# A new order for the start of a two-layer graph transformer: input loads on another queue, step 0 normalised row tile by row tile, neighbour flags by TensorE

## The chip, the cores and the metric

The kernel runs on one core of one Trainium2 chip. The metric is the device time of one execution in microseconds. TensorE is called PE in the profile, VectorE DVE, ScalarE ACT, GpSimd POOL and SyncE SP; SPq and ACTq are the parts of SyncE and ScalarE that issue transfers.

## The reference, cut to what matters

There are 64 graphs of 256 nodes with 512 features, and a 256x256 adjacency mask for each graph. Two layers follow each other, and each adds an attention over the neighbours to its input:

```
h = relu(layernorm(x));  x = x + L0(h, adj)     # 4 heads of 64; a node without a neighbour weighs all nodes alike
h = relu(layernorm(x));  x = x + L1(h, adj)     # a second layernorm inside (gamma, beta), 8 heads of 64, mask = adj or the diagonal
L0: softmax(where(adj, q k^T / 8, -max)) v @ Wo + bo         with q, k, v = h Wq, h Wk, h Wv
L1: softmax(where(adj | eye, q k^T / 8, -1e9)) v @ w_out^T + b_out   with q, k, v = h @ w_qkv^T
```

All values are float32; the mask comes as one byte per element.

## The kernel before

**Steps.** Two graphs are worked on at a time, so there are 32 steps of four row tiles of 128 nodes (`t`), and the 512 features are four chunks of 128 (`c`). All tiles of a step are 128 partitions by 512 elements for one row tile or one chunk.

**One step.** `load_h` brings x into the tile `h` (L476 for step 0, one load for each row tile; L478 for the others, one load of 1 MB) and the mask into `ad` (L480). `norm0` takes mean and variance of a row tile on DVE (`moments`, L547 and L548); with the last row tile, POOL works out one scale `r` and one offset `mr` for each row (`row_scales`, L555 to L559, a power of -0.5), and `scale_row` applies them. `transpose_h` turns the rows on PE, chunk by chunk, and the copy out of PSUM on ACT applies the relu (L619). `act_sums0` and `act_sums1` form four sums of blocks of the result on POOL. `project_qk` makes q and k with seven products of eight matmuls (called `n` = 1, 6, 5, 2, 7, 3, 4 in their order; a scheme with seven products in place of eight), which need sums of the weights too (`weight_sum`, L403). Each product is added up by DVE or ACT (`evacuate`, L630 to L642). The products 2 and 1, 4 and 7, 3 and 5 share a PSUM bank: product 4 is added into the bank of product 7, and only after that bank has been read. `project_v0` makes v for each row tile. `scores`, `mask_scores` (DVE, L807), `exponentials` (ACT, L812), `key_halves` (POOL, L820), `weigh` (PE, L829 and L849), `invert` (DVE, L859) and `normalise` (POOL, L876) are the attention of a pair of heads; the inverted sums go through eight small transfers (L871). `combine0` applies `Wo` to a row tile and adds x (tile `xt`, loaded by `load_x`, L485, with the bias added by `first_bias` on POOL). Layer 1 follows in the same way: `norm1`, `norm1_rest`, `scale_row`, `transpose_h` with gamma and beta, `project_qk`, `project_v1`, four pairs of heads, `combine1` and `store`.

**The neighbour flags.** `neighbours` reduces the mask to one flag for each node (L504). `spread_neighbours` spreads the flags over all partitions: one transfer writes them to DRAM, four bytes at a time (L511), and a second reads them back with a step of zero over the partitions (L513, tile `ne`). `masks` (POOL, L533 to L542) and the copies of products 3 and 4 (L706) use `ne`.

**The order.** Each piece of work is put on a list by `at(period, place, function)`; `at_dense` and `at_set` add a product at one place and its copy out of PSUM at the end of its slot. The list is sorted by `period * 6.13 + place`, and PE, DVE, ACT and POOL execute their instructions in just that order. SP is not among these four: its transfers are put in an order by the framework. Transfers issued by ACT (`nc.scalar.dma_start`) stand in ACT's list at their place. In what follows a place is counted from the start of the list of step 0: `load_h(0)` is at -0.43, `project_qk` of step 0 at 3.57 to 4.57, `load_h(1)` at 3.2, `load_x(0)` at 3.9, `norm0(1, t)` at 4.0, 4.2, 4.4 and 4.6, `project_qk` of step 1 at 5.5, and the first product of layer 1 of step 0 at 12.26. From there on each period has the same pieces of work.

**Loads of the weights.** `first_weights` loads Wq and Wk on SP (tile `wqk0`, four loads L428), and Wv, Wo, the two biases, gamma and beta on ACT. `weight_loads` loads 4 MB of layer-1 weights on ACT, at place 3.5 (four loads L455 into tiles called `wr`, which lie in the space of tiles that come later; one of them lies in the space of an `xt`). `weight_block` turns a quarter of such a load on PE, and DVE and ACT copy it (sixteen blocks, L461 and L466).

**Tiles.** A tile waits for its space until the tile that had it before is no longer read. There is one `h`, one `ad` and one `ne`, and there are two `xt`.

Of the kernel before, what the change touches and what calls it, by code (L numbers as in the profile page):

```python
# [8 lines left out]
FP = mybir.dt.float32  # L9
BF = mybir.dt.bfloat16  # L10
U8 = mybir.dt.uint8
I32 = mybir.dt.int32
AF = mybir.ActivationFunctionType
ALU = mybir.AluOpType

EPS = 1e-5
# [299 lines left out]
def fast_path(  # L316
# [19 lines left out]
    nc = tc.nc  # L336
# [38 lines left out]
    offdiag = const.tile([P, G, P], BF, name="offdiag")  # L375
    for g in range(G):
        nc.vector.tensor_scalar(offdiag[:, g, :], ident, -1.0, 1.0, op0=ALU.mult, op1=ALU.add)
    ones = const.tile([P, 32], FP, name="ones")
    nc.vector.memset(ones, 1.0)
    mhalf = const.tile([P, NT], FP, name="mhalf")  # L380
# [27 lines left out]
    def act_sums1(b, eng=nc.gpsimd):  # L408
        eng.tensor_tensor(b[:, 4], b[:, 2], b[:, 3], ALU.subtract)
        eng.tensor_tensor(b[:, 5], b[:, 2], b[:, 7], ALU.subtract)  # L410
        eng.tensor_tensor(b[:, 6], b[:, 1], b[:, 4], ALU.subtract)
# [13 lines left out]
    def first_weights():  # L425
        for i in range(2):
            for k, w in enumerate((wq, wk)):
                nc.sync.dma_start(  # L428
                    wqk0[:, 2 * i:2 * i + 2, :, k, :].rearrange("p j c o -> p (j c) o"),
                    w[:, i * H0:(i + 1) * H0].rearrange("(c p) o -> p c o", p=P),  # L430
                )
        nc.scalar.dma_start(wv0, wv.rearrange("(c p) o -> p c o", p=P))
        nc.scalar.dma_start(wo0, wo.rearrange("(c p) o -> p c o", p=P))
        for v, t in ((bo, bo_b), (b_out, bout_b)):
            nc.scalar.dma_start(t, bass.AP(tensor=v.tensor, offset=v.offset, ap=[[0, P], [1, D]]))
        gbr = sm.tile([2 * NC, P], FP, name="gbr", tag="inv", bufs=1)
        nc.scalar.dma_start(gbr[:NC], gamma.rearrange("(c p) -> c p", p=P))
        nc.scalar.dma_start(gbr[NC:], beta.rearrange("(c p) -> c p", p=P))
        return gbr
# [6 lines left out]
    def weight_loads():  # L446

        pair = act.tile([P, 2, 4, D], FP, name="wr", tag="oT1")
        blocks = [
            pair[:, 0], pair[:, 1],  # L450
            act.tile([P, 4, D], FP, name="wr", tag="v1"), io.tile([P, 4, D], FP, name="wr", tag="xt"),
        ]
        for n, wr in enumerate(blocks):
            src, r0 = (w_qkv, 4 * n) if n < 3 else (w_out, 0)
            nc.scalar.dma_start(wr, src[r0 * P:(r0 + 4) * P].rearrange("(r p) i -> p r i", p=P))  # L455
        return blocks

    def weight_block(wr, n, c):
# [46 lines left out]
            st["any"][:, rows], st["ad"][:, rows], axis=mybir.AxisListType.X, op=ALU.max  # L505
        )

    def spread_neighbours(s):

        row = dram.tile([NT, P], FP, name="row")  # L510
        nc.sync.dma_start(row.rearrange("t p -> p t"), S[s]["any"])  # L511
        ne = S[s]["ne"] = act.tile([P, T], FP, name="ne")
        nc.sync.dma_start(ne, bass.AP(tensor=row.tensor, offset=row.offset, ap=[[0, P], [1, T]]))  # L513

    def adjacency_turn(s):
        adb = S[s]["adb"]
# [43 lines left out]

    def scale_row(s, t):
        h, r, mr = S[s]["h"], S[s]["r"][:, t:t + 1], S[s]["mr"][:, t:t + 1]
        if s == 0 and t % 2:
            nc.vector.tensor_scalar(h[:, t, :], h[:, t, :], r, mr, op0=ALU.mult, op1=ALU.add)
        else:
            nc.scalar.activation(h[:, t, :], h[:, t, :], AF.Identity, bias=mr, scale=r)  # L566

    def norm0(s, t):
        st = S[s]
        if t == 0:  # L570
            st["mean"] = stat.tile([P, NT, 2], FP, name="mv0", bufs=2)
        moments(st["mean"], st["h"], t)
        if t == NT - 1:
            ve = stat.tile([P, NT], FP, name="ve0", bufs=2)
            nc.gpsimd.tensor_scalar(
                ve, st["mean"][:, :, 1], EPS, 1.0, op0=ALU.add, op1=ALU.mult
            )
            row_scales(s, ve)
# [29 lines left out]
    def transpose_h(s, lyr, c):  # L608
        st = S[s]
        if c == 0:  # L610
            st["hT"] = act.tile([P, NB + 1, HC, N], FP, name="hT")
        ph = mm_tile([P, G, N])
        pv = ph.rearrange("p g n -> p (g n)")
        for t in range(NT):
            nc.tensor.transpose(pv[:, t * P:(t + 1) * P], st["h"][:, t, c * P:(c + 1) * P], ident)  # L615
        b0, b1, step = B_OF[c // HC]
        dst = st["hT"][:, b0:b1:step, c % HC, :]
        if lyr == 0:
            nc.scalar.activation(dst, ph, AF.Relu)  # L619
        else:  # L620
            nc.scalar.activation(
                dst, ph, AF.Identity, bias=gb[:, 1, c:c + 1], scale=gb[:, 0, c:c + 1]
            )

    def evacuate(n, bank, region):

# [259 lines left out]
    def at(period, place, fn, *args):  # L886
        events.append((period * PERIOD + place, len(events), fn, args))
# [48 lines left out]
    for s in range(NSTEP):  # L936

        p = s - 2
        if s == 1:
            p -= 3.93 / PERIOD  # L940
        at(p - 1 if s != 1 else -2, 5.7 if s != 1 else 3.2, load_h, s)
        at(p, (2.9, 2.4)[s] if s < 2 else 0.2, adjacency_cast, s)
        for t in range(NT):
            at(p, 0.5 + 0.4 * t if s != 1 else 1.8 + 0.2 * t, norm0, s, t)
            at(p, 2.3 + 0.1 * t if s != 1 else 2.6 + 0.1 * t, scale_row, s, t)
        for g in range(G):
            at(p, (1.8, 2.7)[s] if s < 2 else 0.58 + 0.14 * g, neighbours, s, g)
        at(p, (1.81, 2.71)[s] if s < 2 else 0.75, spread_neighbours, s)
        at(p, (3.146, 3.584)[s] if s < 2 else 2.2, adjacency_turn, s)
        at(p, (3.3, 3.727)[s] if s < 2 else 2.75, masks, s)  # L950
        for c in range(NC):
            at(p, AT_C0 + 0.14 * (c // 2) + 0.001 * c, transpose_h, s, 0, c)
        at(p, AT_C0 + 0.1, lambda s=s: act_sums0(S[s]["hT"]))
        at(p, AT_C0 + 0.2, lambda s=s: act_sums1(S[s]["hT"]))
        at_set(p, AT_Q0 if s != 1 else 3.3, SET, project_qk, s, 0, 0)
        for t in range(NT):
            at_dense(p, AT_V0 + 0.14 * t, 0.14, project_v0, s, t)
        p = s - 1
        if s == 0:
            p -= 2.23 / PERIOD  # L960
        at(p, 1.0 if s else 0.0, load_x, s)
        at(p, 1.8 if s else 0.8, first_bias, s)
        for t in range(NT):
            at_dense(p, AT_C0 + 0.01 + 0.14 * t, 0.14, combine0, s, t)
            at(p, AT_C0 + 0.3 + 0.14 * t, norm1, s, t)
            at(p, (3.55, 3.7, 4.05, 4.2)[t], norm1_rest, s, t)
            at(p, 3.62 + 0.08 * t, second_bias, s, t)
            at(p, 4.5 + 0.1 * t, scale_row, s, t)

        for c in range(NC):  # L970
            at(p, AT_H1 + 0.0001 * c, transpose_h, s, 1, c)
        at(p, AT_C1 + 0.15, lambda s=s: act_sums0(S[s]["hT"]))
        at(p, AT_C1 + 0.5, lambda s=s: act_sums1(S[s]["hT"]))
        p = s
        at_set(p, 0.0, SET, project_qk, s, 1, 0)
        at_set(p, 1.0, SET, project_v1, s)
        at_set(p, 2.0, SET, project_qk, s, 1, 1)
        at(p, 4.55, lambda s=s: act_sums0(S[s]["oT1"], engine_of(s, 1, 1)))
        if s < NSTEP - 1:
            at(p, AT_C1 + 0.1, lambda s=s: act_sums1(S[s]["oT1"]))  # L980
            at_set(p, AT_C1, SETC, combine1, s)
            at(p, 6.3, store, s)
        else:
            at(p, AT_C1 + 0.4, lambda s=s: act_sums1(S[s]["oT1"], nc.vector))
            at_set(p, AT_C1, (1, 5, 2, 3, 6, 7, 4), combine1, s)
            for n, (i, j) in enumerate(((0, 0), (0, 1), (1, 1), (1, 0))):
                at(p, AT_C1 + (3, 6, 6, 7)[n] / 7, store_block, s, i, j)
# [1 line left out]
    gbr, blocks = [], []  # L989
    at(-3, 5.71, lambda: gbr.append(first_weights()))  # L990
    for i in range(4):
        at(-2, 2.75, weight_sum, nc.vector, wqk0, i)
    at(-2, 3.5, lambda: blocks.extend(weight_loads()))
    at(-2, AT_V0 + 0.2, lambda: gamma_beta(gbr[0]))
    for i in range(16):
        place = 3.3 - 3.93 + 1 / 7 - 0.0005 if i < 4 else 0.2 + 0.07 * i if i < 8 else 1.34 + 0.1 * (i - 8)
        at(-1, place, lambda i=i: weight_block(blocks[i // 4], i // 4, i % 4))
    for i in range(4):
        at(-1, 0.1 + 0.01 * i, weight_sum, nc.vector, wqkv1[:, :, :, 0, :], i)
        at(-1, 1.0 + 0.01 * i, weight_sum, nc.vector, wqkv1[:, :, :, 1, :], i)  # L1000
        at(0, 0.2 + i / 7, weight_sum, nc.vector, wqkv1[:, :, :, 2, :], i)
        at(0, 1.3 + 0.5 * i, weight_sum, nc.gpsimd, wo1, i)
    for _, _, fn, args in sorted(events, key=lambda e: e[:2]):
# [53 lines left out]
```

## Time and profile before

| | |
|---|---|
| median of 9 runs | 3429.93 us (3428.49 to 3436.54) |
| the profiled execution | 3429.1 us |
| its span (first to last instruction) | 3427.3 us |
| mean granted TensorE clock | 0.996 |
| PE busy | 3379.1 us, 99% of the span |
| DVE, ACT, POOL busy | 55%, 36%, 58% |

PE is busy almost everywhere. The execution's own time is 1.8 us more than its span. The windows show the granted clock in each stretch of time; 1.00 is full speed.

### The profile page before, as it was taken

The page shows a single profiled execution, that of the slowest core. Times are in us where ns is not written, and L with a number is a line of the kernel's source. Part 1 is how long each engine was busy: PE and PEld are TensorE (multiplying, and loading weights), DVE is VectorE, ACT ScalarE, POOL GpSimd, SP SyncE. Part 2 cuts the span into 40 slices and gives each one's busy share as a digit, 9 for nine tenths or more (in the row PEclk, how much of TensorE's full clock was granted, in tenths as well). Part 3 has the DMA queues.
Part 4 walks back from the last instruction along what each step waited for, and adds up shares of the span by engine and source line. Part 5 has one row for each costly group of instructions (what it writes and reads, how often), then busy time and mean ns, then how long its engine had stood idle before and what let it go on. Part 6 is the DMA issues. An engine that isn't in the chain of part 4 may idle for free.

```text
span 3427.3 us, 59200 instructions
## 1 busy us (share of the span) xinstructions
PE 3379.1 (99%) x22594; PEld 2625.1 (77%) x22594; DVE 1898.3 (55%) x3377; ACT 1245.0 (36%) x2197; POOL 1991.1 (58%) x1854
## 2 busy tenths in 40 slices
PE   7999999999999999999999999999999999999998
PEld 5787777877777877777777778777777777787766
DVE  4655555555565555555555655555555556555554
ACT  3433443333433334433334333344333443333421
POOL 4556665556655556655566555566555665555641
PEclk9999999999999999999999999999999999999999
DMA  4121111111112111111211112111111111111011
GB/s 134 42 58 51 34 47 56 56 57 52 35 45 58 58 52 34 47 56 56 57 52 34 46 57 58 53 33 47 56 56 57 54 33 46 57 58 51 21 42 38
DMA packets 169041, 174.42 MB, mean 51 GB/s; under 512 B 60712, under 2 KB 113456, under 8 KB 168752
## 3 DMA queue, kind: packets, MB, share of 16 engines
q1 hardware_dynamic: 165344, 164.67, 16.5%
q10 hardware_dynamic: 3408, 5.90, 0.5%
q8 instruction: 180, 2.95, 0.4%
q14 instruction: 109, 0.89, 0.1%
HBM read 86.51 MB, written 33.62 MB: 35 GB/s over the span
## 4 chain that ended last, share of the span: by engine, by line
PE 96%; DMA 1%; DVE 1%; POOL 1%; SPq 0%; issue 0%; ACT 0%; ACTq 0%; DVEq 0%; POOLq 0%
PE mm L696 34%; PE mm L737 11%; PE mm L762 11%; PE sc L794 10%; PE sc L829 10%; PE mm L723 6%; PE mm L748 6%; PE mm L615 3%; PE mm L849 2%; PE mm L521 0%; SPq L871 0%; DMA h<-in_x_dram 0%; DMA invb<-inv 0%; DMA row<-any_of 0%; DVE bs L547 0%
## 5 line engine op out<-in xcount | busy, mean ns | idle before, releaser
L820 POOL TENSOR_TENSOR pd<-p 128x512 f32<-128x512 f32 x380 | 478.4, 1274 | 654.7 <-ACT p L812 543.0
L696 PE MATMUL mm<-hT,wqkv 128*128 128x256 f32 x3584 | 797.2, 381 | 0.0
L696 PEld LDWEIGHTS mm<-hT,wqkv 128*128 128x128 f32 x3584 | 673.3, 190 | 108.8 <-issue 21.0
L812 ACT ACTIVATE p<-p 128x512 f32<-128x512 f32 x768 | 458.8, 629 | 465.8 <-DVE p L807 464.8
L859 DVE RECIPROCAL inv<-mm 128x128 f32<-128x128 f32 x384 | 339.8, 926 | 372.9 <-PE mm L849 333.1
L807 DVE TENSOR_TENSOR p<-sc,n 128x512 f32<-128x512 f32 x768 | 481.1, 682 | 5.0 <-PE sc L794 5.0
L843 ACT COPY oT<-sc 128x512 f32<-128x512 f32 x192 | 112.5, 586 | 1005.1 <-PE sc L829 992.0
L696 PE MATMUL mm<-hT,wqk 128*128 128x256 f32 x1792 | 404.3, 383 | 7.5 <-DVE wqk L403 5.1
L876 POOL TENSOR_TENSOR oT<-oT,invb 128x512 f32<-128x512 f32 x190 | 242.4, 1276 | 276.0 <-DMA invb<-inv 263.5
L762 PE MATMUL mm<-wo,oT 128*128 128x256 f32 x1792 | 393.9, 380 | 5.4 <-ACT u L649 2.2
L696 PEld LDWEIGHTS mm<-hT,wqk 128*128 128x128 f32 x1792 | 339.4, 191 | 77.3 <-issue 14.6
L737 PE MATMUL mm<-wqkv,hT 128*128 128x256 f32 x1792 | 395.3, 381 | 0.0
L794 PE MATMUL sc<-qk 64*128 64x256 f32 x3072 | 385.8, 390 | 2.2 <-ACT oT L843 1.4
L829 PE MATMUL sc<-p,v 128*32 128x256 f32 x6144 | 376.8, 384 | 5.8 <-ACT p L812 5.8
L737 PEld LDWEIGHTS mm<-wqkv,hT 128*128 128x128 f32 x1792 | 337.8, 190 | 55.2 <-issue 10.6
L762 PEld LDWEIGHTS mm<-wo,oT 128*128 128x128 f32 x1792 | 337.9, 190 | 52.5 <-DVE oT L876 2.8
L794 PEld LDWEIGHTS sc<-qk 64*128 64x128 f32 x3072 | 282.2, 187 | 107.3 <-issue 77.3
L829 PEld LDWEIGHTS sc<-p,v 128*32 128x32 f32 x6144 | 181.8, 110 | 171.2 <-issue 62.4
L664 POOL TENSOR_TENSOR xt<-xt,u 128x512 f32<-128x512 f32 x93 | 118.0, 1270 | 244.4 <-DVE xt L657 183.9
L566 ACT ACTIVATE h<-h,mr,r 128x512 f32<-128x512 f32 x252 | 197.5, 809 | 123.6 <-POOL mr L559 123.6
L723 PE MATMUL mm<-wv,hT 128*128 128x256 f32 x1024 | 230.3, 382 | 0.1
L748 PE MATMUL mm<-wo,oT 128*128 128x512 f32 x512 | 230.4, 593 | 0.0
(100 smaller groups left out, 3648.2 us busy)
## 6 DMA issues: line engine op xcount, KB each, us to landing
invb<-inv SPq DMA_DIRECT2D x1532, 32.0 KB, 1.8
xt<-in_x_dram SPq DMA_DIRECT2D x32, 1024.0 KB, 5.5
h<-in_x_dram SPq DMA_DIRECT2D x31, 1024.0 KB, 5.4
out_dram<-xt SPq DMA_DIRECT2D x31, 1024.0 KB, 4.5
ne<-row SPq DMA_DIRECT2D x32, 256.0 KB, 4.1
ad<-in_adj_dram SPq DMA_DIRECT2D x32, 128.0 KB, 11.6
wr<-in_L_gnn_w_qkv_dram ACTq DMA_DIRECT2D x3, 1024.0 KB, 8.9
h<-in_x_dram SPq DMA_DIRECT2D x4, 256.0 KB, 3.1
```

The source lines that it names most:

```text
L696: nc.tensor.matmul(bank[:, k, :], w[:, wa, c, k, a * P:(a + 1) * P], st["hT"][:, ba, c, :], start=first and (k, c) == (0, 0), stop=(k, c) ...
L723: nc.tensor.matmul(bank, st["hT"][:, b0 + t // NIC * step, c % HC, i:i + P], wv0[:, c, :], start=(c == 0), stop=(c == NC - 1),)
L737: nc.tensor.matmul(bank[:, t, :], st["hT"][:, ba, c, t * P:(t + 1) * P], wqkv1[:, wa, c, 2, :], start=first and (t, c) == (0, 0), stop=(t, ...
L748: nc.tensor.matmul(bank, st["oT0"][:, pr, t // NIC, t % NIC * P:(t % NIC + 1) * P], wo0[:, pr, :], start=(pr == 0), stop=(pr == PR0 - 1),)
L762: nc.tensor.matmul(bank[:, t, :], st["oT1"][:, ba, c, t * P:(t + 1) * P], wo1[:, wa, c, :], start=first and (t, c) == (0, 0), stop=(t, c) ...
L794: nc.tensor.matmul(sc[g][e][:, kc, :], qk[rows, 1, k0:k0 + P], qk[rows, 0, g * N:(g + 1) * N], start=True, stop=True,)
L807: nc.vector.tensor_tensor(p[e][:, g], sc[e], neg[:, :, g, :], ALU.add)
L812: nc.scalar.activation(p[e][:, g], p[e][:, g], AF.Exp, scale=SCALE)
L820: engine_of(s, lyr, pr).tensor_tensor(pd[:, e], p[e][:, :, 0, :], p[e][:, :, 1, :], ALU.add)
L829: nc.tensor.matmul(po[r0:r0 + 32, g, :], st[f"v{lyr}"][:, g * NIC + kc, pr * P + r0:pr * P + r0 + 32], p[r0 // DH][:, g, kc, :], start=(kc ...
L859: nc.vector.reciprocal(inv[:, i * P:(i + 1) * P], sums[:, i * P:(i + 1) * P])
L876: engine_of(s, lyr, pr).tensor_tensor(dst, dst, invb, ALU.mult)
```

## The change

Five things are changed. Nothing is changed in what is computed.

1. **Queues.** Wv, Wo, both biases and the four loads of layer-1 weights go from ACT to SP; gamma and beta stay on ACT. `weight_loads` goes from place 3.5 to 4.0, behind `load_x(0)` at 3.9.
2. **Norm and transposes of step 0.** Each row tile gets its scale and offset by itself: DVE adds eps, POOL takes the power of 128x1, DVE makes the offset, ACT scales the row tile. `first_transposes` turns the rows in the order of the row tiles into four banks; two banks are copied by ACT and two by DVE. `scale_row` uses ACT alone; before, DVE scaled the odd row tiles of step 0 in both layers.
3. **Flags of steps 0 and 1.** `neighbours_turn` multiplies a tile of ones by the flags (DVE, four instructions of 128x128), turns it with four matmuls, and copies the result (ACT). From step 2 on, the write and the read of the flags stay, as two pieces of work at places 0.75 and 1.9 (before, both were at 0.75).
4. **Places around the first combination.** `combine0(0)` goes ahead of `project_v0(1, 2)` and `project_v0(1, 3)`; what follows it (`norm1`, `norm1_rest`, `scale_row`) is 0.13 earlier. The weight blocks 1 to 3 are put between products of step 1; blocks 8 to 15 lie at 1.62 to 2.15 (before 1.34 to 2.04).
5. **Other places.** `transpose_h(1)` goes ahead of `weigh(0, 0, 0)`, `project_v0(0, 0)` ahead of `scores(0, 0, 0)`, `adjacency_turn(0)` behind the first two products, `first_bias(0)` to behind the second `key_halves`, and the sums of the k part of the layer-1 weights from 1.0 to 3.1.

```diff
+    onesb = const.tile([P, P], BF, name="onesb")
+    nc.vector.memset(onesb, 1.0)
...
-        nc.scalar.dma_start(wv0, wv.rearrange("(c p) o -> p c o", p=P))
-        nc.scalar.dma_start(wo0, wo.rearrange("(c p) o -> p c o", p=P))
+        nc.sync.dma_start(wv0, wv.rearrange("(c p) o -> p c o", p=P))
+        nc.sync.dma_start(wo0, wo.rearrange("(c p) o -> p c o", p=P))
         for v, t in ((bo, bo_b), (b_out, bout_b)):
-            nc.scalar.dma_start(t, bass.AP(tensor=v.tensor, offset=v.offset, ap=[[0, P], [1, D]]))
+            nc.sync.dma_start(t, bass.AP(tensor=v.tensor, offset=v.offset, ap=[[0, P], [1, D]]))
...
-            nc.scalar.dma_start(wr, src[r0 * P:(r0 + 4) * P].rearrange("(r p) i -> p r i", p=P))
+            nc.sync.dma_start(wr, src[r0 * P:(r0 + 4) * P].rearrange("(r p) i -> p r i", p=P))
...
-    def spread_neighbours(s):
-
-        row = dram.tile([NT, P], FP, name="row")
-        nc.sync.dma_start(row.rearrange("t p -> p t"), S[s]["any"])
+
+    def neighbours_out(s):
+        S[s]["row"] = dram.tile([NT, P], FP, name="row")
+        nc.sync.dma_start(S[s]["row"].rearrange("t p -> p t"), S[s]["any"])
+
+    def neighbours_in(s):
+        row = S[s].pop("row")
         ne = S[s]["ne"] = act.tile([P, T], FP, name="ne")
         nc.sync.dma_start(ne, bass.AP(tensor=row.tensor, offset=row.offset, ap=[[0, P], [1, T]]))
+
+    def neighbours_turn(s):
+
+        rows = act.tile([P, NT, P], BF, name="rows", tag="n0")
+        for t in range(NT):
+            nc.vector.tensor_scalar(rows[:, t, :], onesb, S[s]["any"][:, t:t + 1], None, op0=ALU.mult)
+        pn = mm_tile([P, T])
+        for t in range(NT):
+            nc.tensor.matmul(
+                pn[:, t * P:(t + 1) * P], rows[:, t, :], identb, start=(t == 0), stop=(t == NT - 1),
+                skip_group_check=True,
+            )
+        ne = S[s]["ne"] = act.tile([P, T], FP, name="ne")
+        nc.scalar.copy(ne, pn)
...
-        if s == 0 and t % 2:
-            nc.vector.tensor_scalar(h[:, t, :], h[:, t, :], r, mr, op0=ALU.mult, op1=ALU.add)
-        else:
-            nc.scalar.activation(h[:, t, :], h[:, t, :], AF.Identity, bias=mr, scale=r)
+        nc.scalar.activation(h[:, t, :], h[:, t, :], AF.Identity, bias=mr, scale=r)
...
         moments(st["mean"], st["h"], t)
-        if t == NT - 1:
+        if s == 0:
+            if t == 0:
+                st["r"] = stat.tile([P, NT], FP, name="r", bufs=3)
+                st["mr"] = stat.tile([P, NT], FP, name="mr", bufs=3)
+            r, mr = st["r"][:, t:t + 1], st["mr"][:, t:t + 1]
+            ve = stat.tile([P, 1], FP, name="ve0", bufs=2)
+            nc.vector.tensor_scalar(ve, st["mean"][:, t, 1:2], EPS, None, op0=ALU.add)
+            nc.gpsimd.tensor_tensor(r, ve, mhalf[:, t:t + 1], ALU.pow)
+            nc.vector.tensor_scalar(mr, st["mean"][:, t, 0:1], r, -1.0, op0=ALU.mult, op1=ALU.mult)
+            nc.scalar.activation(st["h"][:, t, :], st["h"][:, t, :], AF.Identity, bias=mr, scale=r)
+        elif t == NT - 1:
...
+    def first_transposes():
+
+        st = S[0]
+        st["hT"] = act.tile([P, NB + 1, HC, N], FP, name="hT")
+        ph = [mm_tile([P, G, N]) for c in range(NC)]
+        for t in range(NT):
+            for c in range(NC):
+                nc.tensor.transpose(
+                    ph[c][:, t // NIC, t % NIC * P:(t % NIC + 1) * P],
+                    st["h"][:, t, c * P:(c + 1) * P], ident,
+                )
+        for c in range(NC):
+            b0, b1, step = B_OF[c // HC]
+            dst = st["hT"][:, b0:b1:step, c % HC, :]
+            if c % 2:
+                nc.vector.tensor_scalar(dst, ph[c], 0.0, None, op0=ALU.max)
+            else:
+                nc.scalar.activation(dst, ph[c], AF.Relu)
...
-        at(p, (2.9, 2.4)[s] if s < 2 else 0.2, adjacency_cast, s)
+        at(p, (2.0, 2.4)[s] if s < 2 else 0.2, adjacency_cast, s)
...
-        at(p, (1.81, 2.71)[s] if s < 2 else 0.75, spread_neighbours, s)
-        at(p, (3.146, 3.584)[s] if s < 2 else 2.2, adjacency_turn, s)
-        at(p, (3.3, 3.727)[s] if s < 2 else 2.75, masks, s)
+        if s < 2:
+            at(p, (3.857, 3.59)[s], neighbours_turn, s)
+        else:
+            at(p, 0.75, neighbours_out, s)
+            at(p, 1.9, neighbours_in, s)
+        at(p, (3.716, 3.583)[s] if s < 2 else 2.2, adjacency_turn, s)
+        at(p, (3.87, 3.74)[s] if s < 2 else 2.75, masks, s)
...
-            at_dense(p, AT_V0 + 0.14 * t, 0.14, project_v0, s, t)
+            at_dense(p, AT_V0 + 0.14 * t + (-0.0005 if s == 0 and t == 0 else 0 if s != 1 else -0.26 if t < 2 else 0.29), 0.14, project_v0, s, t)
...
-        at(p, 1.8 if s else 0.8, first_bias, s)
+        at(p, 1.8 if s else 1.55, first_bias, s)
+        back = 0.0 if s else 0.13
         for t in range(NT):
-            at_dense(p, AT_C0 + 0.01 + 0.14 * t, 0.14, combine0, s, t)
+            at_dense(p, AT_C0 + 0.01 + 0.14 * t - back, 0.14, combine0, s, t)
...
-        at(-2, 2.75, weight_sum, nc.vector, wqk0, i)
-    at(-2, 3.5, lambda: blocks.extend(weight_loads()))
+        at(-2, 3.01, weight_sum, nc.vector, wqk0, i)
+    at(-2, 4.0, lambda: blocks.extend(weight_loads()))
...
-        place = 3.3 - 3.93 + 1 / 7 - 0.0005 if i < 4 else 0.2 + 0.07 * i if i < 8 else 1.34 + 0.1 * (i - 8)
+        place = 3.3 - 3.93 + (1 + i) / 7 - 0.0005 if i < 4 else 0.2 + 0.07 * i if i < 8 else 1.62 + 0.075 * (i - 8)
...
-        at(-1, 1.0 + 0.01 * i, weight_sum, nc.vector, wqkv1[:, :, :, 1, :], i)
+        at(-1, 3.1 + 0.01 * i, weight_sum, nc.vector, wqkv1[:, :, :, 1, :], i)
```

## The prediction

> **What bounds the kernel now.** I read the windows first, cut at the start, the steady part and the end (columns: stretch, its length, busy time of PE, weight loads, DVE, ACT and POOL with counts, granted clock, share and rate of the transfers).
>
> ```profile
> 0.00:110.00 110.00, 84.13 (x505) 62.81 (x505) 53.28 (x101) 39.93 (x82) 54.92 (x63) 0.95 0.39 121
> 500.00:1000.00 500.00, 500.00 (x3384) 391.21 (x3377) 275.12 (x488) 182.82 (x321) 294.65 (x273) 1.00 0.18 51
> ```
>
> From 110 us on PE never stops, so whatever the change does to steps 2 and later on other queues (flags written and read at two places) moves nothing. Only the first 110 us can: PE is idle for 25.9 us there and works some 5 us at half clock. PE's timeline shows where:
>
> ```profile
> 13.46 3.60 PE L615 MATMUL mm<-ident,h 128*128 128x128 f32 x16 [13.46 <-ACT h L566]
> ...
> 24.42 11.73 PE L696 MATMUL mm<-hT,wqk 128*128 128x256 f32 x40 [5.13 <-DVE wqk L403]
> 37.31 1.97 PE L696 MATMUL mm<-hT,wqk 128*128 128x256 f32 x8 [1.17 <-DVE qk L636]
> ```
>
> PE waits 13.5 us for the first rows, 5.1 us for the weight sums, and then 1.2 us at 37.31, which is product 4 of step 0. The third is the one that counts. DVE's timeline says why:
>
> ```profile
> 34.89 0.69 DVE L547 BATCH_NORM_STATS2 bs<-h 128x6 f32<-128x512 f32 x1 [3.19 <-DMA h<-in_x_dram]
> ...
> 36.51 0.66 DVE L636 TENSOR_TENSOR qk<-mm,qk 128x512 f32<-128x512 f32 x1
> ```
>
> DVE's list has the statistics of step 1's first row tiles ahead of the copy of product 7 (L636), whose bank product 4 needs. So product 4 starts 2.42 us after h(1) has landed, however early the rest is done. Last, SP's timeline and the chain of waits:
>
> ```profile
> 13.61 0.37 SPq L480 DMA_DIRECT2D ad<-in_adj_dram  x1
> 22.29 0.34 SPq L513 DMA_DIRECT2D ne<-row  x1
> 22.80 1.03 SPq L478 DMA_DIRECT2D h<-in_x_dram  x1
> ```
> ```profile
> 12.59 9.64 DMA row<-any_of
> 22.29 0.34 SPq L513
> 22.80 12.07 DMA h<-in_x_dram
> ```
>
> The flags' write takes 9.6 us, SP stands behind it, and h(1) then shares the engines with 4 MB of weights from ACT's queue. SP also sent ad(1) at 13.61 ahead of ne, which stands before it in the program: it takes first what has its tile free.
>
> **Part by part.**
>
> *Up to product 3: off the path.* Statistics (0.69 + 0.18), two small DVE instructions (no row; 0.1 to 0.2 each, from the 0.18 aggregates), POOL's power of 128x1 (no row; 0.2, POOL's small adds, to 1.03, the 128x4 power; I take 0.6) and four hand-overs of about 0.08 make 1.6 to 2.6 us a row tile, one after another, since DVE's next statistics stand behind the offset that waits for POOL. From a first row at 3.5 (3.87 before, at shared rate) the fourth is scaled (0.76) at 11 to 14.7. Four transposes (0.11, at half clock 0.22) and the copies give product 1 at 12.5 to 16.5. The weight sums, now behind those copies, are three times 0.73 to 0.97, so product 6 starts at 15.5 to 19.5 in place of 24.42. Products 6, 5, 2, 7, 3 (1.75 each, the first at up to 3.5), the mask's turn (0.45) and the flags' four matmuls (0.06 to 0.11 each) end at 25 to 31. All of this is hidden as long as h(1) comes later than 28.5; if it doesn't, the range above sets the start of product 4.
>
> *h(1).* SP issues what has its tile free: behind the first weights come x(0) and the four weight loads, all into free tiles, while `h` is free only after the last transpose. Each issue waits for a landing eight loads back (L428 at 8.36 is Wo, 1.25 + 7.1), which here comes by 12 us. So I put h(1) last. Bytes ahead: h, Wv and Wo 2.10 MB; Wq, Wk, ad and biases 1.70; x(0) and weights 5.24; ad(1) 0.13; h(1) 1.05. Rates: 385 GB/s (3 to 8 us), 294 (8 to 13, the small rows), 391 (25 to 39). 0.156 MB are through at 3.0, then 5.0 + 5.8 + 16.1 + 0.5 = 27.4, and 0.75 for the landing (x(1): last bytes 103.4, landed 104.15): **31.1** in place of 34.87. At 391 throughout it is 29.7; with another 1.5 us lost between loads, 32.6. Product 4: 31.1 + 2.42 = 33.5, **-3.8** (-5.2 to -2.3).
>
> The Trainium skill ("DMA: Bandwidth & Descriptors", Queues, rings and completion order) speaks against this part: an engine round-robins between the rings of two queues, so on ACT's queue the weights would leave h(1) half the rate, and in one ring it stands behind them all. The trace agrees with the first half: 1 MB took 12.1 us beside the weights, 5.4 alone. With the weights left on ACT, issued at 13 beside h(1), this would give about 22 for its landing.
>
> *Product 4 to step 1's product 1.* Before, 58.16 - 37.31 = 20.85. PE has then been idle for 3 to 8 us, and the clock drops: before, 5.1 us idle gave 6.8 us at 0.50 (2.9 us lost), a shorter stop at 94.9 gave 3.4 us (1.6 lost). I take 2.3 lost. The path: product 4 and v(0,0) 3.45 + 2.3; first half of the scores 1.0; mask 1.3; the fourth statistics 0.9; second mask 1.3 and exponentials 1.2; then ACT scales four rows (0.81 each) with two copies of v between (0.36) and hand-overs, 4.1; last 13 transposes 1.45; weigh 1.86, sums 0.43, scores 1.93. Sum 21.4 with the waits between: **+0.6** (-1.7 without the clock, +1.5). So `transpose_h(1)`, put ahead of `weigh`, waits about 2 us for the rows; first_bias, 4.96 us of POOL, leaves the sums' path, which held PE for 0.61.
>
> The clock gate by the Trainium skill ("TensorE: Matmul & The Clock Gate", Part 1) needs one busy window of about 3.4 us; by that alone 1.7 us are lost and the sum is 0.6 us less.
>
> *Step 1's product 1 to layer 1 (58.16 to 110.07).* Before, PE loses 1.28 + 0.66 at the weight blocks, 1.6 by the clock in the scores, 1.09 at the transposes: 4.6. The combination now ends two v (3.45) earlier against the same work, and single blocks between products wait less. But the four scales on ACT, with block 15's copies (0.6) and an exponential pair (1.2) between, take 5.05 from offset to last row, where ACT and DVE took 2.84 (101.39 to 104.23). PE then waits 3 to 5 us for the last row and runs 1.6 to 2.9 at half clock behind it. Flags of step 1: +0.3. I get -3.45 + 2.2 for the path, -1.0 for the blocks, +1.7 clock, +0.3: **-0.2** (-3 to +3). The k sums (2.93 on DVE) go behind the masks of step 1, 8 us ahead of their first reader.
>
> Sum: -3.8 + 0.6 - 0.2 = **-3.4**, from 3429.1 to 3425.7. That execution is 0.8 under the median, so the median becomes **3426.5**. By the ends alone, 3419 to 3432; its own likely range is 3421 to 3431. 0.2% is 6.9 us, about what a measurement of this kernel can tell from no change.
>
> **The rivals.** *A, SP sends h(1) as soon as its tile is free* (program order has it ahead of x(0) and the weights). Then it lands at 20 to 22, DVE never waits for it, and product 4 starts when product 3 ends, 28.5 (25 to 31): -8.8. PE doesn't stop, the clock holds: -1.7. With -0.2 that is -10.7: 3419. For it: the program order; against: ad(1) at 13.61, sent ahead of two earlier loads. The same if only two weight loads precede it (25.6).
>
> *B, slower: one queue does not carry it.* If 10.1 MB behind one queue move at the rate of the small rows' worst window (240 GB/s, 11 to 12 us), h(1) lands at 3.0 + 42 + 0.75 = 45.7, product 4 at 48.1, +10.8, with the rest 3441. It decides below 268 GB/s (landing after 41.3). For it: those windows, in which rows of 512 bytes and of one repeated source pass; against: x(1) alone on SP moved at 340 to 397.
>
> *C, the tail is worse:* the layer-1 scales on ACT and a cold clock take all of 3 + 1.5 + 1.5 us more than I count. That gives 3430 to 3433, no change.
>
> **How the numbers follow.** The likeliest case has 0.60, A 0.18, B 0.09, C and the like 0.13. Faster by over 0.2%: nearly all of A, and 0.08 of the first case (h(1) at 29.7 and a short cold clock): 0.25. Slower: B, and 0.05 of C: 0.14. Within: 0.61. The range, 3416 to 3435, takes in A with its bounds, C, and leaves out B.
>
> **What would show it.** SP's timeline: the four `wr` issues between 8 and 12 us, h(1) after them, at 13 or later. Windows: 290 to 390 GB/s without a break from 3 to 30. PE: a wait of 3 to 8 us ahead of product 4, released by DVE's copy of product 7, at 33.5; granted clock 0.50 for 3 to 6 us after it; PE solid from 107 on. No row or ne transfer before 100 us. I am wrong if h(1) is issued among or ahead of the weights, if the transfers fall under 270 GB/s, or if PE's first stop of over 2 us after 25 lies elsewhere.

## The result, and the profile after

| | before | changed |
|---|---|---|
| median | 3433.17 us (30 runs, 3427.66 to 3437.28) | 3423.22 us (10 runs, 3420.96 to 3424.8) |
| profiled execution, its span | 3429.1, 3427.3 | 3424.99, 3423.2 |

The ratio of the times is 0.9972, with a 95% interval of 0.9964 to 0.998: faster by 0.28%. The two profiled executions differ by 4.1 us, the medians by 10.0, and both numbers have to be explained. The kernel before had medians from 3428.7 to 3433.2 in the measurements of this study, so kernels of different measurements are compared by their ratios and by three marks on PE's timeline: P4, the start of product 4 of step 0 (where the view has merged it with products ahead of it: the start of v behind it less 1.74); P1, the first product of step 1; L1, the first product of layer 1. From L1 to the end of the span it is 3317.2 before and 3317.3 after, as the prediction had it: all that changed lies ahead of L1. (L1 of the changed kernel is 105.90 on PE's timeline; the expectations below say 105.97, its place in the chain of waits.)

The windows (stretch, length, busy time of PE, weight loads, DVE, ACT, POOL, granted clock, share and rate of the transfers), and the part of PE's timeline that holds step 0:

```profile
0.00:110.00 110.00, 93.03 (x532) 69.17 (x533) 65.47 (x124) 46.10 (x91) 59.60 (x65) 0.95 0.37 120
```
```profile
13.25 3.78 PE L741 MATMUL mm<-hT,wqk 128*128 128x256 f32 x8
18.95 3.75 PE L741 MATMUL mm<-hT,wqk 128*128 128x256 f32 x8 [1.92 <-DVE wqk L405]
...
26.06 7.13 PE L741 MATMUL mm<-hT,wqk 128*128 128x256 f32 x32
33.03 1.89 PE L768 MATMUL mm<-wv,hT 128*128 128x256 f32 x8
```

Product 4 is the last quarter of the 32 matmuls at 26.06: PE runs into it from product 3, P4 is 31.3 (37.31 before), and the wait of 1.17 us for DVE is gone. Products 1 and 6 take 3.78 and 3.75 us where 1.9 is usual: they ran at half clock. The clock column does not show that, because the trace's clock records begin only at 24.77; ahead of the first record the column reads 1.00, and the durations are the better witness.

DVE's and SP's timelines say why product 4 no longer waits, and the list of transfers (last column: us from issue to landing) when h(1) came:

```profile
26.65 0.68 DVE L566 BATCH_NORM_STATS2 bs<-h 128x6 f32<-128x512 f32 x1
...
29.77 0.69 DVE L681 TENSOR_TENSOR qk<-mm,qk 128x512 f32<-128x512 f32 x1 [1.43 <-PE mm L741]
```
```profile
9.43 0.43 SPq L487 DMA_DIRECT2D xt<-in_x_dram  x1
12.44 0.38 SPq L482 DMA_DIRECT2D ad<-in_adj_dram  x1
13.27 0.54 SPq L480 DMA_DIRECT2D h<-in_x_dram  x1
13.86 4.75 SPq L457 DMA_DIRECT2D wr<-in_L_gnn_w_qkv_dram  x3
```
```profile
h<-in_x_dram SPq DMA_DIRECT2D x1, 1024.0 KB, 8.8
```

SP issued h(1) behind x(0) and ahead of the four weight loads (the fourth, of `w_out`, at 18.65), and it landed at 22.1 (13.27 + 8.8). The statistics at 26.65 waited for nothing but their turn.

The chain of waits of the changed kernel no longer has the flags' write or h(1) in it:

```profile
14.10 1.38 DVE wqk L405
15.49 1.65 DVE wqk L405
17.17 1.65 DVE wqk L405
18.81 0.14 issue
18.95 3.75 PE mm L741 x8
```

What was won by then is partly given back. Step 1 up to layer 1, in the timelines of PE, DVE and POOL:

```profile
57.61 0.23 PE L527 MATMUL mm<-identb,rows 128*128 128x128 bf16 x1 [0.99 <-DVE rows L524]
58.83 0.25 PE L527 MATMUL mm<-identb,rows 128*128 128x128 bf16 x1 [0.99 <-DVE rows L524]
59.01 3.54 PE L874 MATMUL sc<-p,v 128*32 128x256 f32 x32
...
97.21 3.03 PE L641 MATMUL mm<-ident,h 128*128 128x128 f32 x13 [1.42 <-ACT h L582]
100.17 3.44 PE L874 MATMUL sc<-p,v 128*32 128x256 f32 x32
...
105.90 9.33 PE L741 MATMUL mm<-hT,wqkv 128*128 128x256 f32 x42
```
```profile
23.42 0.73 DVE L524 TENSOR_SCALAR rows<-onesb,any_of 128x128 bf16<-128x128 bf16 x4
...
54.33 4.44 DVE L524 TENSOR_SCALAR rows<-onesb,any_of 128x128 bf16<-128x128 bf16 x4
```
```profile
55.02 4.93 POOL L493 TENSOR_TENSOR xt<-xt,bo_b 128x512 f32<-128x512 f32 x4
```

The four DVE instructions for the flags of step 1 take 4.44 us beside POOL's adds, the last one of `key_halves` and then those of `first_bias`; in the trace each of the four ends 0.05 to 0.06 us after one of these adds. In step 0, where POOL stands idle beside them, they took 0.73 (23.42). PE waits twice for them, its clock falls, and the weigh behind takes 3.54 in place of 1.93. Ahead of layer 1 it waits again for rows on ACT, and 13 transposes and a weigh run at half clock. P1 to L1 takes 56.4 us, 51.9 before.

### The profile page after: what moved, and what is told of

Read it like the earlier page. It is cut to its first block, busy times and chain, and to the rows that moved or that the text cites. A ratio compares the mean times of both kernels' runs of the same rounds, so it can differ in the third digit from the quotient of the medians.

```text
span 3423.2 us, 59225 instructions
## 1 busy us (share of the span) xinstructions
PE 3383.7 (99%) x22602; PEld 2627.7 (77%) x22602; DVE 1906.7 (56%) x3392; ACT 1248.0 (36%) x2201; POOL 1990.5 (58%) x1854
## 4 chain that ended last, share of the span: by engine, by line
PE 97%; DVE 1%; ACT 0%; SPq 0%; DMA 0%; issue 0%; POOL 0%; ACTq 0%; DVEq 0%; POOLq 0%
PE mm L741 34%; PE mm L782 11%; PE mm L807 11%; PE sc L839 11%; PE sc L874 10%; PE mm L768 6%; PE mm L793 6%; PE mm L641 3%; PE mm L894 2%; PE mm L540 0%; SPq L916 0%; DVE inv L904 0%; ACT h L582 0%; DMA invb<-inv 0%; DVE bs L566 0%
```

## The experiments

All start from the changed kernel unless said otherwise. The spans after L1 lie between 3317.0 and 3318.3 in all profiles but two (3316.7 and 3319.5), so L1 stands for the time of the profiled run.

| kernel | P4 | P1 | L1 | median | ratio to before (95%) |
|---|---|---|---|---|---|
| before | 37.3 | 58.2 | 110.1 | | |
| before, second profile | 36.6 | 58.2 | 112.1 | | |
| changed | 31.3 | 49.4 | 105.9 | 3423.22 | 0.9972 (0.9964 to 0.998) |
| changed, second measurement | 28.4 | 46.6 | 100.1 | 3420.98 | 0.997 (0.9958 to 0.9982) |
| h(1) behind the weights | 34.7 | 54.6 | 109.1 | 3428.59 | 0.9989 (0.998 to 0.9998) |
| first_bias later | 29.8 | 48.0 | 100.0 | 3420.06 | 0.9965 (0.9951 to 0.9979) |
| flags by DRAM | 29.8 | 51.3 | 101.6 | 3419.58 | 0.9964 (0.9951 to 0.9978) |
| norm of step 0 at once | 27.3 | 45.6 | 101.9 | 3419.23 | 0.9962 (0.9948 to 0.9975) |
| loads on ACT | 33.0 | 51.2 | 106.1 | 3424.78 | 0.9982 (0.9973 to 0.9991) |
| weight sums early | 29.4 | 47.6 | 102.2 | 3421.57 | 0.9973 (0.9963 to 0.9983) |
| combination at old places | 30.0 | 48.2 | 110.1 | 3428.37 | 0.9994 (0.9985 to 1.0003) |
| odd rows on DVE too | 30.1 | 48.3 | 99.2 | 3419.52 | 0.9974 (0.9965 to 0.9983) |
| three edits together | 27.4 | 45.7 | 95.1 | 3415.88 | 0.9965 (0.9951 to 0.9978) |
| four, and a busy start | 27.5 | 45.8 | 95.2 | 3414.3 | 0.9944 (0.9931 to 0.9958) |

The measurements were made on several chips. By the ratios, of the single edits only the combination at its old places, and just barely h(1) behind the weights, can be told from the changed kernel (0.9964 to 0.998); what is said of the others rests on the waits and marks of one profile each.

**The changed kernel again (no edit).** 

> The changed kernel, unchanged, once more: the other kernels were timed on other chips, on which the kernel before has medians between 3428.7 and 3433.2. Theory, the chips differ for the kernel before (its PE stops of 1 to 5 us fall against the clock's windows in more than one way) and less for the changed one: the changed kernel at 3421 to 3425, ratio 0.997 to 0.9985. Rival, the ratio of the first measurement, 0.9972, holds within 0.0005 whatever the chip.

```profile
18.93 1.97 PE L741 MATMUL mm<-hT,wqk 128*128 128x256 f32 x8 [1.92 <-DVE wqk L405]
...
56.12 1.93 PE L874 MATMUL sc<-p,v 128*32 128x256 f32 x32
...
95.61 2.20 PE L874 MATMUL sc<-p,v 128*32 128x256 f32 x32
```

The ratio held and the rival was nearer. The profile is the lesson (PE's timeline): with the same waits to 0.01 us, product 6 and the two weighs ran at full or nearly full clock, and L1 came 5.8 us earlier. The profiled execution of the first measurement was the slowest of its runs. A single profile of this kernel is therefore good to some 6 us at L1, and what follows counts waits first and clock second.

**Before again (the kernel before, no edit).** 

> The kernel before, unchanged, profiled a second time, since its profiled execution (3429.1) lies under the median of later runs (3433). Theory, its time depends on where PE's stops fall in the clock's windows of 3.4 us in the first 110 us: here product 4, step 1's first product and layer 1 start 1 to 5 us later than 37.31, 58.16 and 110.07, with the flags' write still 9 to 12 us long, and the rest of the span (3317.2 from layer 1 on) is the same. Rival, the rest of the span varies: landmarks within 0.5 us and the difference behind 3000 us.

 P4 came 0.75 earlier, P1 0.1 later and L1 2.0 later, for one more stretch of 3.41 us at half clock, under the transposes and the weigh ahead of it; so the theory holds for L1 alone, and the rest of the span was 0.5 shorter. That execution took 3430.6. The gap between 4.1 and 10.0 comes from where the two profiled executions lie among their runs: the one before is 4.1 under its median (3429.1 and 3433.17), the changed one 1.8 over its own (3424.99 and 3423.22). That the clock's windows are what brings executions of the kernel before to 3433 is argued, not shown, since no execution of that length was profiled.

**h(1) behind the weights.** This run makes the order that the prediction held for likeliest.

```diff
-    at(-2, 4.0, lambda: blocks.extend(weight_loads()))
+    at(-2, 3.1, lambda: blocks.extend(weight_loads()))
-        at(p, 1.0 if s else 0.0, load_x, s)
+        at(p, 1.0 if s else -0.85, load_x, s)
```

> The changed kernel, with x(0) and the four loads of layer-1 weights put ahead of h(1) on SP's queue (the case that the prediction held for likeliest). Theory, the place of h(1) in the queue sets product 4 of step 0 as soon as it lands late: h(1) lands at 31.1 (29.7 to 32.6) in place of 22, product 4 starts 2.42 us later, at 33.5 (32 to 35) in place of 31.4, PE stops for 2 us ahead of it, the first product of layer 1 comes 2 to 4 us later, 108 to 110 in place of 105.97, and the time is 3425 to 3427. Rival, the early start of product 4 comes from the norm and transposes alone and h(1) has slack of 9 us: product 4 stays at 31.4, layer 1 at 106.0, the time at 3423.

DVE's and PE's timelines:

```profile
32.25 0.69 DVE L566 BATCH_NORM_STATS2 bs<-h 128x6 f32<-128x512 f32 x1 [8.32 <-DMA h<-in_x_dram]
```
```profile
34.68 3.62 PE L741 MATMUL mm<-hT,wqk 128*128 128x256 f32 x8 [6.01 <-DVE qk L681]
```

The theory holds for the path: h(1) came at 32.25, product 4 started 2.43 us later, and L1 lies in its bounds. PE stood longer than it said, 6.0 us in place of 2, and then worked at half clock; the time is 1.6 us over its bounds. Against the changed kernel's two profiles L1 is 3.2 and 9.0 us later, and most of the gain is gone (ratio 0.9989).

**first_bias later.**

```diff
-        at(p, 1.8 if s else 1.55, first_bias, s)
+        at(p, 1.8 if s else 2.1, first_bias, s)
```

> The changed kernel, with first_bias of step 0 (4.93 us of adds on POOL) put behind the masks of step 1, so that it no longer lies beside the four DVE instructions that spread the flags of step 1. Theory, each of these four waits for a POOL add (1.1 to 1.2 us each there, 0.18 alone in step 0): they take 0.2 each, the two PE waits of 0.99 us go, the clock stays up in the weigh behind them (3.54 in place of 1.93 us), and layer 1 starts 3 to 4.4 us earlier, at 101.6 to 103, time 3419 to 3420.5. Rival, the four are slow for another reason or PE waits for the next thing instead: layer 1 at 105 to 106, time 3422.5 to 3423.5.

```profile
52.87 1.27 DVE L524 TENSOR_SCALAR rows<-onesb,any_of 128x128 bf16<-128x128 bf16 x4
```
```profile
55.16 1.93 PE L874 MATMUL sc<-p,v 128*32 128x256 f32 x32
...
69.54 1.99 PE L768 MATMUL mm<-wv,hT 128*128 128x256 f32 x8 [0.61 <-DVE qk L685]
```

The theory holds for the cause: with `first_bias` elsewhere the four take 1.27 us, and both PE waits are gone. The first of them still stands beside an add of `key_halves` and ends 0.06 us after it; the other three go as fast as in step 0. P1 to L1 takes 52.0, against 56.4 and 53.5: 4.4 less than the profile with the fallen clock, 1.5 less than the one without (two waits of 0.99 less a new one of 0.61).

**Flags by DRAM.**

```diff
-            at(p, (3.857, 3.59)[s], neighbours_turn, s)
+            at(p, (1.81, 2.71)[s], neighbours_out, s)
+            at(p, (1.81, 2.71)[s], neighbours_in, s)
```

> The changed kernel, with the flags of steps 0 and 1 sent through DRAM as before (the write and the read at their old places). Theory, the flags by TensorE bring nothing in step 0, where POOL needs them at 27, and cost 4 us in step 1: product 4 at 31 to 32, step 1 loses two waits of 0.99, 0.8 of matmuls and 1.6 of clock, layer 1 at 101.5 to 103, time 3418.5 to 3420.5. Rival, the DRAM way holds up SP's queue: the write takes 9.6 us, ne stands behind h(1), masks of step 0 come at 30 or later and scores of step 0 wait: product 4 or the scores later by 3 or more, layer 1 at 107 or later, time 3424 to 3429.

SP's, POOL's and PE's timelines:

```profile
13.25 0.37 SPq L480 DMA_DIRECT2D h<-in_x_dram  x1
24.22 0.34 SPq L518 DMA_DIRECT2D ne<-row  x1
```
```profile
31.16 2.29 POOL L555 TENSOR_TENSOR n<-n,ne 128x512 bf16<-128x512 bf16 x2 [5.89 <-DMA ne<-row]
```
```profile
35.97 3.47 PE L839 MATMUL sc<-qk 64*128 64x256 f32 x16 [2.53 <-POOL qk L751]
```

Both are half right. The theory's L1 and time were met, but in step 0 the flags by TensorE do bring something: by DRAM POOL gets them at 31.2 in place of 27, the scores wait 2.5 us and lose the clock, and P4 to P1 takes 21.5 in place of 18.2. In step 1 they cost: P1 to L1 takes 50.3 by DRAM. Against the second profile of the changed kernel the two nearly cancel (3.3 lost, 3.2 won). The flags' write did not hold up h(1) here: SP sent h(1) at 13.25, ahead of the read of the flags, which stands before it in the program.

**Norm of step 0 at once.**

```diff
-        if s == 0:
+        if s < 0:                      # norm0: the new branch for step 0 is not taken
...
-            at(p, AT_C0, first_transposes)
+            at(p, AT_C0 + ..., transpose_h, s, 0, c)   # and scale_row of step 0, odd rows on DVE
```

> The changed kernel, with the norm and the transposes of step 0 done as before: one scale for the four row tiles together, odd row tiles scaled by DVE, transposes by chunk with all four copies on ACT. Theory, the norm by row tile starts product 1 three to four us earlier (13.25), but PE then works at half clock until 24.8 and waits 1.9 us for the weight sums, so that most of it is lost again: product 1 at 16 to 17.5 at full clock (1.9 us), product 4 at 28.5 to 32, time 3420 to 3425. Rival, the norm by row tile is where the gain is: product 4 at 35 or later, time 3427 or more.

```profile
10.66 3.68 PE L644 MATMUL mm<-ident,h 128*128 128x128 f32 x16 [10.66 <-ACT h L585]
14.18 1.89 PE L744 MATMUL mm<-hT,wqk 128*128 128x256 f32 x8
...
27.35 1.97 PE L744 MATMUL mm<-hT,wqk 128*128 128x256 f32 x8 [0.89 <-DVE qk L684]
```
```profile
11.39 2.86 DVE L405 TENSOR_TENSOR wqk<-wqk 128x512 f32<-128x512 f32 x4
```

The rival falls: the old way gives an earlier P4 (27.35) than the norm by row tile (28.4 and 31.3), earlier even than the theory's bounds. With the transposes in one piece PE's clock is up for product 1. DVE adds up the weights ahead of POOL's sums and takes 0.72 us for each in place of 1.62 (6.46 for four, from 14.02 on, beside POOL adds that take 1.6 to 1.7 in place of 1.27). Only then does product 4 wait for h(1), which lands at 24.9, since SP sent one weight load ahead of it here. The edit changes the norm, the transposes, their copies and with them DVE's order together, so what each of these is worth is not shown.

**Loads on ACT.**

```diff
-        nc.sync.dma_start(wv0, ...)      # and wo0, both biases, wr
+        nc.scalar.dma_start(wv0, ...)
```

> The changed kernel, with Wv, Wo, both biases and the four loads of layer-1 weights issued by ACT again (at the changed place 4.0, behind x(0)). Theory, what freed h(1) is that SP no longer waits for the write of the flags; on which queue the weights lie counts little, since ACT comes to them only behind the flags' copy at 26, when h(1) has landed: h(1) lands at 18 to 23, product 4 at 31 to 32.5, layer 1 at 105 to 107, time 3422 to 3425. Rival, the move to SP is what gains: ACT stands at its issues as before (until 21.44 there), the first scaled row or the copies of the products come 2 to 5 us late, product 4 at 34 or later, time 3426 to 3430.

ACT's and SP's timelines:

```profile
8.60 0.25 ACTq L440 DMA_DIRECT2D gbr<-in_L_gnn_beta_dram  x1
8.95 1.28 ACT L598 ACT_TABLE_LOAD   x1 [8.95 <-DMA h<-in_x_dram]
```
```profile
14.85 0.37 SPq L480 DMA_DIRECT2D h<-in_x_dram  x1
```

Between the two: L1 and the time are the theory's, but ACT stands at its issues until 8.85 and scales its first row at 10.24 (5.55 in the changed kernel), and Wk comes later (DVE's sums start at 16.02). P4 is 33.0, 1.7 later than in the first profile of the changed kernel, which also ran its first products at half clock. So the move to SP is worth some 2 us at the start, and the rest of the early product 4 is not the queue's: SP sent h(1) at 14.85 all the same. With the flags back in DRAM it did so too, at 13.25. So an early h(1) needs neither of these two by itself, and which part of the change made it early stays open.

**Weight sums early.**

```diff
-        at(-2, 3.01, weight_sum, nc.vector, wqk0, i)
+        at(-2, 1.75, weight_sum, nc.vector, wqk0, i)
```

> The changed kernel, with the four sums of Wq and Wk on DVE put ahead of the flags' reduction and of the copies of the transposes, so that they no longer lie beside POOL's adds. Theory, they take 0.7 to 1.0 us each in place of 1.44 to 1.64, PE's wait of 1.92 us behind product 1 goes, PE then works without a break and its clock is up some 2 to 5 us earlier (24.8 in the changed kernel); product 1 comes 1 to 2 us later (15), product 4 at 28 to 30 in place of 31.4, layer 1 at 102.5 to 105, time 3420 to 3422. Rival, what is won at the sums is lost at product 1: product 4 at 31 to 32, time 3423.

```profile
16.46 5.48 PE L741 MATMUL mm<-hT,wqk 128*128 128x256 f32 x14 [2.02 <-DVE hT L666]
```

The sums took 0.88 us each (3.50 for four), but PE's wait only moved: it now stands 2.02 us for DVE's copies of the transposes, which are queued behind the sums. P4 lies between the two profiles of the changed kernel; this settles nothing.

**Combination at old places.**

```diff
-        back = 0.0 if s else 0.13
+        back = 0.0
-  0 if s != 1 else -0.26 if t < 2 else 0.29        # project_v0
+  0
-  (1 + i) / 7 - 0.0005 if i < 4 else ... 1.62 + 0.075 * (i - 8)    # weight_block
+  1 / 7 - 0.0005 if i < 4 else ... 1.34 + 0.1 * (i - 8)
```

> The changed kernel, with the places of the first combination as before: combine0 interleaved with v of step 1, 0.13 later what follows it, weight blocks 1 to 3 together, blocks 8 to 15 at 1.34 to 2.04. Theory by the prediction's sum, the earlier combination is worth 3.45 us less what ACT's scaling of all four rows and the cold clock behind it cost: from step 1's first product to layer 1 it takes 57 to 60 in place of 56.5, layer 1 at 106.5 to 109.5, time 3424 to 3427. Rival, the places bring nothing: the same within 0.5, time 3423.

P1 to L1 takes 61.9, 5.4 more than in the first profile of the changed kernel, whose weighs ran at half clock in the same two places. The theory holds, and the gain was larger than it said: ACT starts on the first row of layer 1 48.2 us after P1 in place of 43.2.

**Odd rows on DVE too.**

```diff
-            at(p, 4.5 + 0.1 * t - back, scale_row, s, t)
+            at(p, 4.5 + 0.1 * t - back, scale_row, s, t, s == 0)   # there: DVE scales odd t
```

> The changed kernel, with the odd row tiles of step 0 in layer 1 scaled by DVE again (ACT scales the even ones). Theory, with ACT alone the last row is ready 4.5 us after the offset (92.65 to 97.15; 2.84 before), PE has 2.6 us of waits there, and its clock falls behind them (13 transposes 3.03, weigh 3.44 in place of 1.45 and 1.93): the last row comes at 94.5 to 95.7, layer 1 1.5 to 4.5 us earlier, at 101.5 to 104.5, time 3418.5 to 3422. Rival, DVE has the masks of step 1 to do there (92.9 to 95.3) and its rows only displace them: weigh waits for its exponentials, layer 1 at 105 to 106.5, time 3423.

```profile
91.96 1.79 PE L644 MATMUL mm<-ident,h 128*128 128x128 f32 x14 [0.74 <-ACT h L585]
93.68 1.93 PE L877 MATMUL sc<-p,v 128*32 128x256 f32 x32
...
96.72 0.63 PE L897 MATMUL mm<-pd,ones 128*32 128x256 f32 x6 [0.69 <-POOL pd L868]
```

The theory holds: PE waits 0.74 us for the rows in place of 2.64, its clock stays up, and P1 to L1 takes 50.9, 2.6 less than in the second profile of the changed kernel and 5.5 less than in the first. A new wait of 0.69 for POOL appears.

**Three edits together** (norm at once, first_bias later, odd rows on DVE; the weight loads stand at 4.3 in place of 4.0). 

> The changed kernel with three of the edits together: norm and transposes of step 0 at once, first_bias behind the masks of step 1, odd rows of layer 1 scaled by DVE. Theory, they act on different waits (before product 4, in the flags of step 1, ahead of layer 1) and add up: 4.0 + 4.5 + 1.5 to 4.5 from 105.97, layer 1 at 93 to 96.5, time 3409 to 3414. Rival, the stretches share waits, above all by the clock, and the sum is half of that: layer 1 at 98 to 101, time 3415 to 3419.

 L1 is 95.1, within the theory's bounds; the time, 3415.9, is 2 us over them and in the rival's. Against the second profile of the changed kernel, the one whose clock fell less, the stretches show that the edits add up: P4 is 1.0 earlier (1.1 with the norm alone), and P1 to L1 takes 4.1 less (1.5 and 2.6 alone). In the same measurement the three have 3414.8 to 3416.0, the odd rows alone 3417.4 to 3422.0.

**Four, and a busy start.** To these three: 60 PE transposes of the identity that nothing reads, and h(1) ahead of most weights, forced by a small DVE write into the weights' tiles.

```diff
+            for _ in range(60):
+                nc.tensor.transpose(pv[:, :P], ident, ident)
+            nc.vector.memset(wr[:, 0, :1], 0.0)        # for each wr, at place 3.3
```

> The three edits together (norm and transposes of step 0 at once, first_bias later, odd rows on DVE) and two more: 60 PE transposes of the identity, read by nothing, ahead of the first ones, and h(1) ahead of three of the four layer-1 weight loads and of x(0). Theory, the clock is up before the first real transposes (16 in 1.8 to 2.0 in place of 3.96, product 1 and the next in 3.6 in place of 4.92), h(1) lands at 20 to 22 in place of 24.9, product 4 starts at 24 to 25.5 in place of 27.44, layer 1 at 92 to 93.5 in place of 95.1, time 3411 to 3414. Rival, the clock rises only with products and not with such transposes, or another wait takes the place of h(1): product 4 at 27, time 3415 to 3417.

Windows, PE, DVE:

```profile
0.00:110.00 110.00, 100.89 (x653) 79.39 (x657) 72.37 (x135) 44.34 (x90) 65.36 (x68) 1.00 0.38 122
```
```profile
1.36 9.44 PE L649 MATMUL mm<-ident 128*128 128x128 f32 x60 [1.36 <-POOL ident masks.py:199]
11.08 2.50 PE L651 MATMUL mm<-ident,h 128*128 128x128 f32 x16 [0.28 <-ACT h L589]
13.42 1.89 PE L751 MATMUL mm<-hT,wqk 128*128 128x256 f32 x8
...
27.53 1.96 PE L751 MATMUL mm<-hT,wqk 128*128 128x256 f32 x8 [1.06 <-DVE qk L691]
```
```profile
25.10 0.69 DVE L570 BATCH_NORM_STATS2 bs<-h 128x6 f32<-128x512 f32 x1 [3.36 <-DMA h<-in_x_dram]
```

The clock theory holds (full from 6.88 on in the trace's records, with no half stretch before 3300), but the rival is right about product 4. The small writes stand behind the weight sums on DVE, so the first weight load and h(1) behind it were issued at 15.65 and 16.13, and h(1) landed at 25.1. L1 is the same as with three edits, which also kept the full clock from 16.96 to 3300 without the busy start. The median, 3414.3, and the ratio, 0.9944, are the lowest of the study: this version beats the kernel before, and, in the same measurement, the changed one (3420.98, its fastest run 3419.2 against 3414.6 for the slowest here). Against the three edits it is not told apart; these were measured at another time, and the intervals overlap.

## Why the prediction was right and wrong

The median fell by 0.28% to 3423.2: inside the range, on the forecast's side, 3.3 us under it, and past the 0.2% that was given a chance of 0.25. The likeliest case, h(1) last, did not happen, and that the number is near is in good part luck. Against the profile before, the forecast of -3.4 met -4.1 in the first profile, because two steps failed in opposite ways; in the second it was -9.9. By the medians it was -10.0, near the -10.7 of rival A, which had a chance of 0.18. The forecast of the time came out near all the same because it started from a median of 3429.9 (9 runs), where the 30 runs of the result have 3433.2.

*h(1), forecast P4 -3.8, measured -6.0 and -8.9.* The failed step is "So I put h(1) last". From ad(1), which had gone ahead of earlier loads, I concluded that SP sends whatever has its tile free. In the changed kernel SP waited 2.6 us at ad(1) and then sent h(1) ahead of the weights, although their tiles were free (with h(1) behind them they went out from 9.74 on): rival A. Program order alone is not the rule either, since x(0), which stands behind h(1) in the program, went ahead of it at 9.43; how the order comes about stays open. The rest of the step was sound: with the order made as forecast, h(1) landed at 32.25 (29.7 to 32.6), product 4 followed after 2.43 (2.42) and PE stood 6 us. Rival A's P4 of 28.5 was met by the second profile (28.4); in the first, product 6, the mask's turn and part of product 5 at half clock made it 31.3.

*Up to product 3: "off the path", 25 to 31.* It was on the path, since h(1) was early; P4 came at 28.4 in one profile and at 31.3, just past the slow end of those bounds, in the other. The sums, put at 0.73 to 0.97, took 1.62 beside POOL's adds. By the Trainium skill ("SBUF — State Buffer", Who interferes with whom) DVE and POOL share a port pair: a DVE instruction in a two-port mode, which a `tensor_scalar` can enter, and the POOL instruction beside it block each other for the whole instruction, and a DVE instruction with two inputs in SBUF contends with a POOL instruction that reads SBUF. The trace agrees for the flags (0.18 us alone, 1.1 beside adds of 1.23). For the sums it is milder than a full lock: 1.62 for a DVE sum and a POOL add, where 0.72 + 1.27 would be 1.99.

*Product 4 to P1, +0.6, measured -2.7 in both profiles.* The term for the cold clock (2.3) fell away with PE's stop. The wait of the transposes (about 2) was mis-sized: it is 0.54 (0.17 and 0.37) in the changed kernel and also with h(1) behind the weights, where PE did stop and the stretch took 19.9 us against a forecast of 21.4.

*P1 to L1, -0.2, measured +4.5, and +1.6 in the second profile.* The failed term is "Flags of step 1: +0.3", a cost taken from step 0's surroundings without a look at what POOL does at that place. It was 2.0 of waits and the matmuls, and 1.6 more of clock in the first profile. Two other terms were mis-sized and went against each other: the places of the combination brought the first scaled row forward by 5.0 (put at 3.45, and 1.0 for the blocks), and from that row to L1 it took 13.2 us (92.65 to 105.90) in place of 8.6 (101.43 to 110.07), +4.6 (put at 2.2 for the rows on ACT and 1.7 for the clock).

*The clock.* I charged it as a fixed price of a stop. The same stops cost 5.8 us more in one profile than in the other. The Trainium skill ("TensorE: Matmul & The Clock Gate", Part 1) calls the window free-running, not reset by a kernel's start; the records agree, with stretches of 3.41 us and multiples whose start differs from run to run. What counts is how long PE stands within one such window. Behind the flags of step 1 both stops of 0.99 us fell into one window of the first profile (55.50 to 58.91, PE idle for 1.98 us), and the next ran at half clock; in the second profile they fell into two (1.27 and 0.71 us), and the clock stayed.

*Two readings.* The 110 us before hold 10.2 us at half clock, as the prediction's own 6.8 and 3.4 say, not "some 5"; 5 us is what was lost. And at 391 GB/s throughout, its sum for h(1) gives 29.5, not 29.7. Neither moves the forecast.

## What to carry to other kernels

Before a DVE instruction is moved, look at what POOL executes at the new place: an instruction of 0.2 us can take the time of the POOL instruction beside it, and PE's clock may fall behind that. Two short stops close together can cost a stretch at half clock that one of them would not, so it pays to remove either. Where PE starts with short pieces and gaps, one dense start can beat an earlier first product (here P4 was 1.1 to 3.9 us earlier, with the weight sums clear of POOL's adds too). Where a queue's order decides a forecast, read the rule off more than one row, and price both orders.

## What the runs showed of the hardware

- One program, two profiles, the same waits: L1 at 100.1 and 105.9, by where PE's stops of 1 to 2 us fell in the clock's windows of 3.41 us.
- In all fourteen profiles, from the first clock record to 115 us, each of the 24 windows at full clock in which PE stood for 1.72 us or more was followed by one at half clock. Of those in which it stood for 1.67 us or less, one was (1.36 us, the second profile of the kernel before). A window at half clock was followed by full clock when PE stood for at most 0.69 us in it, and by another at half clock when it stood for 0.75 us or more (6 windows).
- A DVE instruction of 0.18 us on 16-bit data that met a POOL add of two tensors ended 0.05 to 0.06 us after that add.
- 60 transposes of 128x128 that nothing reads raised the clock at 6.88, after 5.5 us of work: from there on one starts every 0.11 us, before every 0.21.
- Ahead of the first clock record (16.6 to 24.8 us into the span in the two main profiles) the granted clock reads 1.00 while matmuls take twice their time.
